# The last two expert tiles of an attention and mixture-of-experts kernel put behind a runtime condition

## The chip, the cores and the metric

The kernel runs on one core of one Trainium2 chip. The metric is the device time of one execution in microseconds (us). Three runs of the kernel before took 2227.67, 2231.09 and 2233.11 us; the median, 2231.09 us, is what the predicted time is set against.

## The reference

The input is 8 sequences of 1024 tokens with 256 features, all float32. First comes causal attention with 16 heads between two layer norms, with a residual. Then comes a mixture of experts:

```
logits = flat @ router_weight.T + router_bias
scores = softmax(logits);  topk_w, topk_idx = top_k(scores, 2)
gu   = flat @ gate_up_proj[e] + gate_up_bias[e]        # 8 experts, 256 -> 2 x 512
act  = (clip(up) + 1) * gate * sigmoid(1.702 * gate)   # gate cut at 7
down = act @ down_proj[e] + down_bias[e]               # 512 -> 256
out  = sum over the two chosen experts of down * topk_w
x    = x + layernorm(out)
```

The reference computes all experts for all tokens; what matters is each token's two chosen experts, so 8192 tokens make 16384 rows of expert work.

## The kernel before

**Sorting by expert.** While attention runs, `route` ranks the experts of every 512 tokens and scatters each token's normed row twice, into a DRAM buffer `xs_dram` that holds a region for each of the 8 experts. `counts` is how many rows each region has. From the counts, `table` (L279 and on) makes a list of 71 tiles on the chip: for tile i, `tables[..][0, 0, i]` is its expert and `tables[..][0, 1, i]` the row of `xs_dram` where its 256 rows (`TS`) begin. There are two such lists: one for the first 12 tiles (`EARLY`), made when 12 of the 16 groups of tokens are known and holding full tiles only, and one, `tables[NT]`, for the other tiles.

**Why 71.** `NTILES` (L100) is the most tiles that any routing can need: `(8192 * 2 - 8) // 256 + 8`. Each expert rounds its rows up to whole tiles, so the number of tiles with rows is between 64 and 71. A tile of the list that no expert takes gets expert 0 and the row `E * R` = 67584, a block behind all regions.

**One tile.** `load_tile` (L1257) has SyncE (SP) read the two numbers of the list into registers and start four loads: the rows `xs` (258 KB), the gate and up weights `wg` (1024 KB), the biases `bs` (132 KB), the down weights `wd` (512 KB). `turned` (L1284) transposes the rows on TensorE (PE), has ScalarE (ACT) copy them out of PSUM and has VectorE (DVE) work out to which rows of `yt_dram` the results go. `quarter` (L1303), four times, multiplies by a quarter of `wg` (line L1308) and makes a quarter of `act`: DVE takes gate and up out of PSUM (L1317, L1321), ACT does the sigmoid (L1319), GpSimd (POOL) multiplies (L1324), DVE finishes (L1329). `lower_half` (L1335) multiplies by `wd` (L1339), DVE adds the bias (`ys`, L1345), and POOL scatters the 2 x 128 result rows to `yt_dram` by two indirect DMAs (L1349).

**The order of the work.** It is written out by hand for PE, DVE and ACT. In the loop over tiles (L1453) the load of tile i + 2 is started at tile i (`AHEAD`), the transpose of tile i + 1 stands in quarter 2 of tile i, and `lower_half` of tile i - 1 is spread over the quarters of tile i (`behind`).

**The ends.** `both(t)` (L1359) closes group t of 512 tokens: it loads the attention result `x1` and the group's rows `yy` of `yt_dram`, sums the two experts' rows with their weights (ACT L1386, DVE L1391), takes mean and variance (L1395, L1396), the inverse root on POOL (L1403), `shift` on DVE (L1409), scales on ACT (L1416), adds on DVE (L1421), and writes 512 KB of output (L1425). It is a generator; `an_end` (L1449) runs one step of it inside a quarter. `tiles_for(r)` says from which tile on group r's rows are all done: 67 for group 14, 71 for group 15. Group 14's loads are put in the program when tile 67 ends, its steps begin at tile 69 (`i + 2`), and what is left of it runs after the loop. Group 15 (`final`) runs after the loop in any case; its four `yy` loads (L1372) wait for the last tile's scatters.

Of the kernel before, what the change touches and what calls it, by code (L numbers as in the profile page):

```python
# [11 lines left out]
F32 = mybir.dt.float32  # L12
# [5 lines left out]
P = 128  # L18
# [40 lines left out]
def attn_moe_kernel(  # L59
# [15 lines left out]
    nc = tc.nc  # L75
# [11 lines left out]
    E = router_w.shape[0]  # L87
    FF = down.shape[1]
    FT = FF // P
    TB = 512  # L90
    NT = B * S // TB
# [3 lines left out]
    TS = 256  # L95
    TN = TS // P
    R = B * S + TS
    ROWS = E * R + TS

    NTILES = (B * S * TOPK - E) // TS + E  # L100
# [84 lines left out]
    counts = const.tile([P, NT + 1, E], F32, name="counts")  # L185
# [66 lines left out]
    def fill_tails():  # L252
# [14 lines left out]
    tables = {  # L267
        n: const.tile([1, 2, NTILES], I32, name=f"table{n}") for n in (NT - LATE, NT)
    }
# [138 lines left out]
    with ExitStack() as attn:  # L408
# [653 lines left out]
        now = 0  # L1062
# [76 lines left out]
        with tc.manual_schedule(  # L1139
# [11 lines left out]
            for u in range(B * NG + 1):  # L1151
# [12 lines left out]
                for k in range(K):  # L1164
# [15 lines left out]
                    for pair in range(2):  # L1180
# [33 lines left out]
                        if len(late) > DELAY - 1 or (late and not second):  # L1214
                            f, kk = late[0]
# [22 lines left out]
            while late:  # L1238
                f, kk = late.popleft()
# [12 lines left out]
    m2 = pool("moe2", 2)  # L1252
# [4 lines left out]
    def load_tile(i):  # L1257
        tab = tables[NT - LATE if i < EARLY else NT]
        e = loaded(tab[:, 0, i : i + 1], E - 1)
        xs_sb = early.pop(i, None)  # L1260
        if xs_sb is None:
            at = loaded(tab[:, 1, i : i + 1], E * R)
            xs_sb = m4.tile([P, TN, XD], F32, tag="xs", name=f"xs_{i}")
            load = nc.sync.dma_start(out=xs_sb, in_=slot_rows(at))
            if i < EARLY:
                ahead_of(load, "xs")
        wg = m3.tile([P, KT, 2 * FF], F32, tag="wg", name=f"wg_{i}")
        nc.sync.dma_start(
            out=wg, in_=gate_up[ds(e, 1), :, :].rearrange("o (t p) f -> p (o t) f", p=P)
        )  # L1270
        bs = m4.tile([P, 2 * FT + D], F32, tag="bs", name=f"bs_{i}")
        nc.sync.dma_start(
            out=bs, in_=bias_dram[ds(e, 1), :, :].rearrange("o p c -> p (o c)")
        )
        wd = m4.tile([P, FT, D], F32, tag="wd", name=f"wd_{i}")
        nc.sync.dma_start(
            out=wd, in_=down[ds(e, 1), :, :].rearrange("o (t p) d -> p (o t) d", p=P)
        )
        return xs_sb, wg, bs, wd
# [4 lines left out]
    def turned(i, xs_sb):  # L1284
        ps = ps_x.tile([P, KT, TS], F32, tag="x", name=f"xtps_{i}")
        for kt in range(KT):
            for n in range(TN):
                nc.tensor.transpose(ps[:, kt, ts(n, P)], xs_sb[:, n, ts(kt, P)], ident)  # L1288
        xT = m2.tile([P, KT, TS], F32, tag="xsT", name=f"xsT_{i}")
        nc.scalar.copy(xT, ps)  # L1290

        far = m4.tile([P, TN], F32, tag="far", name=f"far_{i}")
        nc.vector.tensor_scalar(
            far, xs_sb[:, :, D], float(B * S * TOPK), float(i * (TS + 1)), ALU.is_ge, ALU.mult
        )
        nc.vector.scalar_tensor_tensor(
            far, xs_sb[:, :, D + 1], regions[NT - LATE if i < EARLY else NT][:, i : i + 1], far,
            ALU.not_equal, ALU.add,
        )
        nc.vector.tensor_tensor(places[:, i, :], far, xs_sb[:, :, D], ALU.add)  # L1300
        return xT

    def quarter(i, f, xT, wg, bs, act):  # L1303

        ps = ps_gu.tile([P, 2, TS], F32, tag="gu", name=f"gu_{i}_{f}")
        for half in range(2):
            for kt in range(KT):
                nc.tensor.matmul(  # L1308
                    ps[:, half, :],
                    lhsT=wg[:, kt, ds(half * FF + f * P, P)],  # L1310
                    rhs=xT[:, kt, :],
                    start=(kt == 0), stop=(kt == KT - 1),
                )
            if half == 0 and i + AHEAD < EARLY:
                pump(0.6, 0.35, 0.6, 0.35)
        gt = m3.tile([P, TS], F32, tag="gate", name=f"gate_{i}_{f}")
        nc.vector.tensor_scalar(gt, ps[:, 0, :], bs[:, f : f + 1], LIMIT, ALU.add, ALU.min)  # L1317
        sg = m3.tile([P, TS], F32, tag="sig", name=f"sig_{i}_{f}")
        nc.scalar.activation(sg, gt, AF.Sigmoid, scale=ALPHA)  # L1319
        up = m3.tile([P, TS], F32, tag="up", name=f"up_{i}_{f}")  # L1320
        nc.vector.tensor_scalar(  # L1321
            up, ps[:, 1, :], bs[:, FT + f : FT + f + 1], LIMIT + 1.0, ALU.add, ALU.min
        )
        in_order(nc.gpsimd.tensor_tensor(sg, sg, gt, ALU.mult))  # L1324
        if i + AHEAD < EARLY:
            pump(0.6, 0.35, 0.6, 0.35)

        def product():
            nc.vector.scalar_tensor_tensor(  # L1329
                act[:, f, :], up, 1.0 - LIMIT, sg, ALU.max, ALU.mult  # L1330
            )

        return product

    def lower_half(i, act, wd, bs):  # L1335
        ps = ps_b.tile([P, TN, D], F32, tag="b", name=f"dn_{i}")
        for n in range(TN):
            for f in range(FT):
                nc.tensor.matmul(  # L1339
                    ps[:, n, :], lhsT=act[:, f, ts(n, P)], rhs=wd[:, f, :],  # L1340
                    start=(f == 0), stop=(f == FT - 1),
                )
            yield
        y = m4.tile([P, TN, D], F32, tag="ys", name=f"ys_{i}")
        nc.vector.tensor_tensor(  # L1345
            y, ps, bs[:, 2 * FT :].unsqueeze(1).to_broadcast([P, TN, D]), ALU.add
        )
        for n in range(TN):
            put = nc.gpsimd.indirect_dma_start(  # L1349
                out=yt_dram[:, :],  # L1350
                out_offset=bass.IndirectOffsetOnAxis(ap=places[:, i, n : n + 1], axis=0),
                in_=y[:, n, :], in_offset=None,
            )
            in_order(put, scatter=True)
            apart(put, "yt")
        yield
# [70 lines left out]
    def tiles_for(r):  # L1427


        return max(((r + 1) * TB * TOPK - E) // TS + E, EARLY + E)  # L1430

    AHEAD = 2
    engines = mybir.EngineType
    with tc.manual_schedule(engines={engines.PE, engines.DVE, engines.Activation}):
        free[0] = False
        loads = {0: load_tile(0)}
        for i in range(IN_X, 2 * IN_X):
            at = loaded(tables[NT - LATE][:, 1, i : i + 1], E * R)
            early[i] = m4.tile([P, TN, XD], F32, tag="xs", name=f"xs_{i}")
            ahead_of(nc.sync.dma_start(out=early[i], in_=slot_rows(at)), "xs")  # L1440
        for i in range(1, AHEAD):
            loads[i] = load_tile(i)
        xTs = {0: turned(0, loads[0][0])}
        behind, left = None, None
        waiting = deque()
        ready = 0
        ends = deque()

        def an_end(i):  # L1449
            if ends and i >= ends[0][0] and next(ends[0][1], "end") == "end":  # L1450
                ends.popleft()

        for i in range(NTILES):  # L1453
            if i + AHEAD == EARLY:
                finish_all()
            if i + AHEAD < NTILES:
                loads[i + AHEAD] = load_tile(i + AHEAD)
            _, wg, bs, wd = loads.pop(i)
            xT = xTs.pop(i)
            act = m2.tile([P, FT, TS], F32, tag="act", name=f"act_{i}")  # L1460
            for f in range(FT):
                now_left = quarter(i, f, xT, wg, bs, act)
                if left:
                    left()
                left = now_left
                for _ in range(2 if f == FT - 1 and i % 2 else 1):
                    an_end(i)
                if f == 1 and behind:
                    next(behind)
                if f == 2:  # L1470
                    if i + 1 < NTILES:
                        xTs[i + 1] = turned(i + 1, loads[i + 1][0])
                    if behind:
                        next(behind)
                        next(behind)
                if i + AHEAD < EARLY:
                    pump(1.2, 0.7, 1.0, 0.7)
            while ready < NT and i >= tiles_for(ready):
                waiting.append(ready)
                ready += 1  # L1480
            if waiting and len(ends) < 2:
                work = both(routed[waiting.popleft()])
                next(work)
                ends.append((i + 2, work))
            behind = lower_half(i, act, wd, bs)
        left()
        for _ in behind:
            pass
        for r in [*waiting, *range(ready, NT)]:
            ends.append((0, both(routed[r], r == NT - 1)))  # L1490
        while ends:
            an_end(NTILES)
        free[0] = True
# [36 lines left out]
```

## Time and profile before

| what | value |
|---|---|
| median of three runs | 2231.09 us (2227.67 to 2233.11) |
| time of the profiled execution | 2227.21 us |
| its span, first to last instruction | 2225.5 us |
| PE busy | 2161.5 us, 97% of the span |
| DVE, ACT, POOL busy | 1647.3, 1090.8, 1067.0 us |
| mean granted PE clock | 0.994 of full speed |
| gate and up matmuls, L1308 | 2272 in 71 tiles, 516.2 us busy |
| down matmuls, L1339 | 1136 in 71 tiles, 273.5 us busy |

The page gives times in us from the start of the span. A busy share is an average over the whole span; a stage is read by cutting the span into windows. The chain of waits follows the execution back from its last instruction, each time to what released it.

The two stages show in the page's forty slices of 55.6 us: in the first 25, attention, the loads move 12 to 59 GB/s after the first slice; in the next 14, the expert tiles, 178 to 273 GB/s; the last holds the end of the tiles and the last group.

### The profile page before, as it was taken

Reading aid. Unit: us, or ns where it says so; the run is one execution under the profiler, and the core shown is the slowest. Engines: PE = TensorE matmul, PEld = TensorE weight load, DVE = VectorE, ACT = ScalarE, POOL = GpSimd, SP = SyncE. Lnnn points to the kernel's source line nnn. Section 1 sums busy time; section 2 is a strip of 40 time slices with the busy share of each in tenths; the row PEclk is TensorE's granted clock in tenths of the full one; section 3 lists DMA queues with packets and bytes.
Section 4 is the critical chain, followed back from the end, with each engine's and each line's share of the span. In section 5 each row is a group of like instructions: output and inputs, shape, how many; then the busy total and the mean of one; then the engine's idle time right before and its main releaser. Section 6 shows DMA issues by size and latency. Waiting matters only on the chain.

```text
span 2225.5 us, 45180 instructions
## 1 busy us (share of the span) xinstructions
PE 2161.5 (97%) x16801; PEld 1347.5 (61%) x16801; DVE 1647.3 (74%) x3770; ACT 1090.8 (49%) x2179; POOL 1067.0 (48%) x1229
## 2 busy tenths in 40 slices
PE   7999999999999999999999999999999999999995
PEld 3444544544544445445445444778888888888885
DVE  4776777867867777877776787676668888887775
ACT  3666665665666666666666666431122322322222
POOL 3421652662573573473472463464444444444543
PEclk9999999999999999999999999999999999999998
DMA  4001102102102111111111111657667778777773
GB/s 106 17 12 35 26 16 55 40 21 59 40 21 55 36 30 38 52 30 31 49 40 23 45 52 40 219 178 253 214 227 269 259 262 273 266 243 273 241 245 124
DMA packets 141363, 251.17 MB, mean 113 GB/s; under 512 B 17664, under 2 KB 103576, under 8 KB 139224
## 3 DMA queue, kind: packets, MB, share of 16 engines
q1 hardware_dynamic: 126968, 212.17, 30.5%
q0 software_dynamic: 12960, 35.54, 4.2%
q8 instruction: 133, 2.18, 0.4%
q14 instruction: 86, 0.70, 0.1%
q10 hardware_dynamic: 1216, 0.58, 0.1%
HBM read 175.74 MB, written 55.76 MB: 104 GB/s over the span
## 4 chain that ended last, share of the span: by engine, by line
PE 81%; DVE 10%; POOL 4%; issue 3%; ACT 1%; DMA 1%; SPq 0%; ACTq 0%; DVEq 0%; POOLq 0%
PE sa L693 20%; PE gu L1308 17%; PE av L825 12%; PE dn L1339 9%; PE sb L788 7%; PE yps L886 3%; PE pjq L600 3%; PE pjk L600 3%; PE vps L586 2%; PE avt L856 1%; DVE acc L1391 1%; PE xtps L1288 1%; DVE gate L1317 1%; DVE act L1329 1%; DVE up L1321 1%
## 5 line engine op out<-in xcount | busy, mean ns | idle before, releaser
L796 ACT ACTIVATE pT<-sb 128x512 f32<-128x512 f32 x1152 | 625.2, 595 | 404.5 <-PE sb L788 375.7
L788 PE MATMUL sb<-qP,kP 32*128 32x512 f32 (+3 forms) x3072 | 710.7, 523 | 2.1 <-DMA qP<-nmT 1.0
L693 PE MATMUL sa<-kP,qP 32*128 32x512 f32 (+3 forms) x3072 | 653.8, 524 | 3.4 <-DVE mx L703 1.4
L1308 PE MATMUL gu<-xsT,wg 128*128 128x256 f32 x2272 | 516.2, 379 | 0.8 <-ACT xsT L1290 0.7
L1308 PEld LDWEIGHTS gu<-xsT,wg 128*128 128x128 f32 x2272 | 430.6, 190 | 59.9 <-ACT xsT L1290 1.4
L805 POOL TENSOR_SCALAR_AFFINE_SELECT pT<-pT 128x512 f32<-128x512 f32 x256 | 160.0, 641 | 592.3 <-ACT pT L796 586.9
L709 DVE TENSOR_REDUCE mx<-sa 128x2 f32<-128x1024 f32 x256 | 311.5, 1219 | 112.2 <-PE sb L788 108.6
L1319 ACT ACTIVATE sig<-gate 128x256 f32<-128x256 f32 x284 | 118.3, 417 | 562.7 <-DVE gate L1317 560.7
L825 PE MATMUL av<-pT,vpad 128*32 128x256 f32 (+1 forms) x5120 | 345.0, 366 | 1.1 <-DVE avs L836 0.9
L1324 POOL TENSOR_TENSOR sig<-sig,gate 128x256 f32<-128x256 f32 x284 | 210.6, 743 | 274.9 <-ACT sig L1319 273.0
L693 PEld LDWEIGHTS sa<-kP,qP 32*128 32x128 f32 x3072 | 227.8, 184 | 188.4 <-issue 97.3
L788 PEld LDWEIGHTS sb<-qP,kP 32*128 32x128 f32 x3072 | 297.6, 184 | 40.9 <-ACT pT L796 7.2
L825 PEld LDWEIGHTS av<-pT,vpad 128*32 128x32 f32 x5120 | 116.4, 108 | 287.2 <-issue 208.0
L1339 PE MATMUL dn<-wd,act 128*128 128x256 f32 x1136 | 273.5, 381 | 8.0 <-DVE act L1329 7.5
L1317 DVE TENSOR_SCALAR gate<-gu,bs 128x256 f32<-128x256 f32 x284 | 135.7, 478 | 154.2 <-PE gu L1308 138.1
L1339 PEld LDWEIGHTS dn<-wd,act 128*128 128x128 f32 x1136 | 208.6, 190 | 40.7 <-DVE act L1329 16.0
L703 DVE CUSTOM_DVE_ANT_0 sa<-sa,cmask 128x512 f32<-128x512 f32 x256 | 178.1, 697 | 51.2 <-PE sb L788 27.0
L1349 POOL DMA_INDIRECT ytd<-ys,places x142 | 142.9, 1006 | 136.5 <-DVE ys L1345 112.3
L1046 POOL DMA_INDIRECT xsd<-xn,slots x128 | 126.9, 992 | 47.0 <-issue 29.4
L718 DVE TENSOR_REDUCE mx<-sa 128x2 f32<-128x512 f32 x128 | 88.1, 689 | 75.5 <-PE sb L788 49.7
L1329 DVE SCALAR_TENSOR_TENSOR act<-up,sig 128x256 f32<-128x256 f32 x284 | 131.7, 464 | 14.5 <-POOL sig L1324 14.5
L1321 DVE TENSOR_SCALAR up<-gu,bs 128x256 f32<-128x256 f32 x284 | 134.5, 474 | 0.0
(204 smaller groups left out, 2399.9 us busy)
## 6 DMA issues: line engine op xcount, KB each, us to landing
wg<-_L_ffn_gate_up_proj_dram SPq DMA_DIRECT2D x71, 1024.0 KB
wd<-in_L_ffn_down_proj_dram SPq DMA_DIRECT2D x71, 512.0 KB
xs<-xsd SPq DMA_DIRECT2D x67, 258.0 KB
yy<-ytd SPq DMA_DIRECT2D x15, 1024.0 KB
bs<-biasd SPq DMA_DIRECT2D x71, 132.0 KB
x<-in_L_attn_x_dram SPq DMA_DIRECT2D x16, 512.0 KB
x1d<-y SPq DMA_DIRECT2D x16, 512.0 KB
x<-x1d SPq DMA_DIRECT2D x16, 512.0 KB
```

Of the source, the lines that this page charges most:

```text
L693: nc.tensor.matmul(ps[:, hh, ds(at, w)], lhsT=qP[r, ts(i, P)], rhs=kP[r, ds(c * QC, w)], start=True, stop=True,)
L703: nc.vector.tensor_tensor_reduce(out=ps[:, hh, :], in0=ps[:, hh, :], in1=cmask, scale=1.0, scalar=NEG, op0=ALU.add, op1=ALU.max, accum_out ...
L709: nc.vector.tensor_reduce(mx[:, heads, i, 2:3], ps, AX.X, ALU.max)
L788: nc.tensor.matmul(banks[hh][:, ds(at, QC - off)], lhsT=kP[r, ts(j, P)], rhs=qP[r, ds(c * QC + off, QC - off)], start=True, stop=True,)
L796: nc.scalar.activation(pT[:, 2 * pair + hh, :], banks[hh], AF.Exp)
L805: in_order(nc.gpsimd.affine_select(out=d, in_=d, compare_op=ALU.is_ge, fill=0.0, base=0, pattern=[[0, HG], [1, P]], channel_multiplier=-1,))
L825: nc.tensor.matmul(av[ds(hh * HS, HS), ds(off + a - at, z - a)], lhsT=vp[:, j, ds((g * HG + hh) * VS, HS)], rhs=pT[:, hh, a:z],  start=c n ...
L1308: nc.tensor.matmul(ps[:, half, :], lhsT=wg[:, kt, ds(half * FF + f * P, P)], rhs=xT[:, kt, :], start=(kt == 0), stop=(kt == KT - 1),)
L1317: nc.vector.tensor_scalar(gt, ps[:, 0, :], bs[:, f : f + 1], LIMIT, ALU.add, ALU.min)
L1321: nc.vector.tensor_scalar(up, ps[:, 1, :], bs[:, FT + f : FT + f + 1], LIMIT + 1.0, ALU.add, ALU.min)
L1324: in_order(nc.gpsimd.tensor_tensor(sg, sg, gt, ALU.mult))
L1339: nc.tensor.matmul(ps[:, n, :], lhsT=act[:, f, ts(n, P)], rhs=wd[:, f, :], start=(f == 0), stop=(f == FT - 1),)
```

## The change

The loop over tiles ends two tiles earlier, at `SURE` = 69, and nothing is loaded or transposed ahead for tiles 69 and 70 in it. Behind the loop, `values_load` has every engine read one number into a register, the row where tile 69 begins by `tables[NT]`. If it is less than `E * R`, tiles 69 and 70 run one after the other by a new function `tile_alone`, without loads ahead and without steps of other work between. Otherwise they are jumped over. What is left of the ends then runs as before.

```diff
+    SPARE = 2
+    SURE = NTILES - SPARE
+
+    def tile_alone(i):
+        xs_sb, wg, bs, wd = load_tile(i)
+        xT = turned(i, xs_sb)
+        act = m2.tile([P, FT, TS], F32, tag="act", name=f"act_{i}")
+        last = None
+        for f in range(FT):
+            now = quarter(i, f, xT, wg, bs, act)
+            if last:
+                last()
+            last = now
+        last()
+        for _ in lower_half(i, act, wd, bs):
+            pass
...
-        for i in range(NTILES):
+        for i in range(SURE):
...
-            if i + AHEAD < NTILES:
+            if i + AHEAD < SURE:
...
-                    if i + 1 < NTILES:
+                    if i + 1 < SURE:
...
         left()
         for _ in behind:
             pass
+        spare = nc.values_load(
+            tables[NT][:, 1, SURE : SURE + 1], min_val=0, max_val=E * R,
+            skip_runtime_bounds_check_because="tables made on the chip from counts of tokens",
+        )
+        with tc.If(spare < E * R):
+            for i in range(SURE, NTILES):
+                tile_alone(i)
         for r in [*waiting, *range(ready, NT)]:
             ends.append((0, both(routed[r], r == NT - 1)))
```

In the built program, each engine's list now has a register load and a compare-and-branch behind tile 68, then the block of the two tiles (51 instructions on DVE, 21 on ACT, 15 on POOL, 23 on SP), then a second block that runs in its place: it raises the semaphores by what the two tiles would have raised them (two instructions on PE, DVE and ACT each, five on POOL, ten on SP), after waits for what came before, and ends with a branch to the rest. On SP those waits are for all its earlier DMAs, on POOL for earlier scatters. The arithmetic steps of group 14, of which tiles 69 and 70 held nearly all, now stand in the rest, behind the branch; its loads stay where they were, in tile 68's time.

## The prediction

> **What bounds the kernel now.** First the page: who is busy, and whose time the chain of waits is made of.
>
> ```profile
> PE 2161.5 (97%) x16801; PEld 1347.5 (61%) x16801; DVE 1647.3 (74%) x3770; ACT 1090.8 (49%) x2179; POOL 1067.0 (48%) x1229
> PE 81%; DVE 10%; POOL 4%; issue 3%; ACT 1%; DMA 1%; SPq 0%; ACTq 0%; DVEq 0%; POOLq 0%
> ```
>
> PE bounds nearly all of it. But the change lies at the end, so I cut the end into stages: tile 68, 69 and 70 (from the end of one tile's third quarter of L1308 to the next's), what is left of tile 70, the trip of its rows to DRAM and back, and the last group.
>
> ```profile
> 2166.80:2177.60 10.80, 10.80 (x54) 9.51 (x53) 7.34 (x17) 2.14 (x5) 5.28 (x7) 1.00 0.72 239
> 2177.60:2188.40 10.80, 10.80 (x54) 9.51 (x53) 8.66 (x22) 3.34 (x8) 4.46 (x6) 1.00 0.47 163
> 2188.40:2199.11 10.71, 10.62 (x50) 9.03 (x48) 8.94 (x22) 2.07 (x5) 6.66 (x8) 1.00 0.07 24
> 2199.11:2205.31 6.20, 4.15 (x17) 2.68 (x15) 2.31 (x6) 2.38 (x5) 2.21 (x3) 1.00 0.12 42
> 2205.31:2213.64 8.33, 0.00 (x0) 0.00 (x0) 1.41 (x5) 0.00 (x0) 1.97 (x2) 0.77 0.48 157
> 2213.64:2225.50 11.86, 0.00 (x0) 0.00 (x0) 6.26 (x20) 4.21 (x8) 1.59 (x2) 0.50 0.25 89
> ```
>
> Columns: length, then busy us of PE, weight loads, DVE, ACT, POOL, then clock, DMA share, GB/s. A tile costs 10.8 us, all of it PE. Then PE is done, and in the fifth stage nearly everything waits for the round trip of the last rows. The timeline shows its ends:
>
> ```profile
> 2204.62 0.69 DVE L1345 TENSOR_TENSOR ys<-dn,bs 128x512 f32<-128x512 f32 x1 [2.52 <-PE dn L1339]
> 2205.59 1.01 POOL L1349 DMA_INDIRECT ytd<-ys,places  x1 [3.95 <-DVE ys L1345]
> 2206.91 0.96 POOL L1349 DMA_INDIRECT ytd<-ys,places  x1 [0.30 <-issue]
> 2210.29 1.74 SPq L1372 DMA_DIRECT2D yy<-ytd  x4
> 2213.64 0.51 ACT L1386 ACTIVATE acc<-yy,chosen_w 128x256 f32<-128x256 f32 x1 [11.30 <-DMA yy<-ytd]
> ```
>
> Call the end of the last tile's `ys` T0. Scatter, landing, load and landing take 2213.64 - 2205.31 = 8.33 us, whatever tile is the last.
>
> **Is the condition false?** No row of the profile tells it: an empty tile loads and computes as a full one does. I worked the routing out from the reference and its inputs. The experts get 1887, 2102, 2059, 1860, 1869, 2468, 1692 and 2447 rows, so 8+9+9+8+8+10+7+10 = 69 tiles of 256. The early list takes only full tiles, so it adds none. Tiles 69 and 70 are empty, and 92 rows would have to change expert before any of these counts passed its next multiple of 256.
>
> **What goes.** Tiles 69 and 70: 10.80 + 10.71 = **21.51 us**, the second and third rows above. The same 8.33 us behind the last tile stays, with tile 68 in tile 70's place. The loads of the two tiles (about 1.9 MB each) go too, but loads were not late there: PE was busy 10.80 of 10.80 us.
>
> **What is added: the branch.** Each engine reads a register from the list, compares, branches, raises semaphores and branches again. The register read has rows on SP:
>
> ```profile
> L244 SPq TENSOR_LOAD <-table x142: 262/275/990, 1319.9 to 2159.0; - x142
> ```
>
> 0.28 us in the median. Raising a semaphore is the 0.02 to 0.05 us of the trace's EVENT_SEMAPHORE records. A taken branch has no row. From below it is about such a record, 0.02 us. From above it is a stop until code has come by DMA, and code does come so:
>
> ```profile
> q8 instruction: 133, 2.18, 0.4%
> q14 instruction: 86, 0.70, 0.1%
> ```
>
> 133 packets carry 2.18 MB, 16 KB each; 86 carry 0.70 MB, 8 KB each. The trace has 34176 records on PE (16801 matmuls, 17375 of weight loads and waits), 257 for each packet of the one kind, and 11004 on the other engines, 128 for each of the other. So code comes in blocks of 256 and 128 instructions. An 8 KB packet takes 0.31 to 0.89 us; with its request I set it at the 2.5 us that a scatter of this stage takes from issue to landing, 2.9 us together, an estimate. Which end? The jump skips 51 instructions on DVE, 21 on ACT, 15 on POOL and 23 on SP, less than half a block, so its target lies in the block that runs or in the next, which straight code needs early as well. I take the lower end, 0.05 us a branch: 0.28 + 2 x 0.05 + 0.05 = 0.43 us an engine, and keep 2 x 2.9 + 0.28 + 0.05 = 6.1 us for the range.
>
> [...]
>
> **What hides it.** On PE nothing follows. SP waits in its second block for all its earlier DMAs; the last of these, `yy` and `x1` of group 14, are issued at 2174.12 and 2175.64, in tile 68. ACT used that `yy` at 2180.48 without a wait, and now 0.6 MB of loads that shared the queue with it are gone. SP's next task is the `yy` load of group 15 at T0 + 4.98, that is 2188.8 in old time: over 8 us of cover. POOL ends its second scatter at T0 + 2.56 and must raise its semaphores before that same load: 2.42 us of cover for 0.5 us (a semaphore raise by the software queue took 0.03 us at the kernel's start). Only DVE and ACT can show it.
>
> **What is moved: group 14.** Its sums lay in tiles 69 and 70, beside PE. Now they come behind the branch, beside the 8.33 us trip. ACT's four `acc` need only `yy` and end before T0: 2180.48 + 4 x 0.52 = 2182.6, against T0 = 2205.31 - 21.51 = 2183.80. From T0 on, with durations of the last group's rows:
>
> - DVE's branch: 0.43
> - four rounds of L1391, L1395, L1396 (2214.19 to 2218.79): 4.60
> - `ve`, then POOL: 0.26 to its start, and 1.04 for `rstd` of four columns (the row at 2194.03): 1.30
> - `shift` and its two hand-overs: 0.30
> - four `o` on ACT (the row at 2200.28, x4): 2.06
>
> Sum 8.69 us; ACT then begins group 15's `acc` at T0 + 8.69 in place of T0 + 8.33, 0.36 late. DVE's fourth addition of group 14 and the stretch of an `acc` beside a scatter (0.76 for 0.48 at 2190.79) add some tenths in one place; I take **0.5 us late** in all. The 512 KB output of group 14 is written under group 15's 11.86 us.
>
> **Sum.** -21.51 + 0.5 = -21.0 us. The profiled execution took 2227.21 us, 1.7 above its span; with the change 2206.2. It was 3.9 us below the median of the runs shown, under their lowest. Set against the median: 2231.09 - 21.0 = **2210.1 us**.
>
> **The rivals.**
>
> *Code stalls at the branches.* One block late on DVE or ACT gives 8.69 + 2.9 - 8.33 + 0.1 = 3.4 us late, 2213.0 us; both late, 6.3 us, 2215.9 us. The same holds if POOL's semaphores come after its 2.42 us of cover. [...] Against: the short jump.
>
> *The tiles run after all* (slower; the change then does not skip what it says). One mechanism: an expert's count passes a multiple of 256, the list has 70 tiles with rows, and both tiles run alone. Loads begin only behind the branch: 1.9 MB at the 268 GB/s of the tile stage, 7.2 us. Each tile is then a chain with nothing beside it: transposes and copy 1.2, four quarters of 1.73, and the 6.20 us of the fourth row above, 14.3 us. Both: 7.2 + 28.6 = 35.8 in place of 21.51, 14.3 us more: about 2245.9 us. It decides from the 70th tile; I count 69.
>
> *The exposed group costs more than a tail.* If DVE ran its rounds at the 0.95 us that L1391 takes in the median beside POOL, four times 0.47 more: 2.4 us late, 2212.0 us. Against: POOL has only two scatters there.
>
> **How the numbers follow.** Forecast 0.78; code stalls 0.13; dearer group 14 0.05; the tiles run 0.03; something else 0.01. Bounds: nothing late gives 2209.6; both blocks late 2215.9. The runs before lie 3.4 below and 2.0 above their median, which I add in part: 2206 to 2217.5. Measurement can tell about 0.3%, 6.7 us, from no change. All cases but the third and last are at least 15 us faster: faster 0.95, same 0.01, slower 0.04.
>
> **What would show it.** 138 instead of 142 scatters of L1349 and 69 loads of `wg`; T0 near 2183.8; on DVE a gap under 0.5 us between `ys` and group 14's first L1391; the `yy` load of L1372 still 4.98 us after T0; group 15's first `acc` at T0 + 8.6 to 8.9. Wrong would be a gap of 2 us or more on DVE, ACT or POOL at the branch, or L1372 late behind POOL.

## The result and the profile after

The changed kernel took 2206.68 us in the median (four runs, 2204.11 to 2212.08); the kernel before, in the same comparison, 2229.38 us (2226.53 to 2233.11). The ratio is 0.9899, 95% interval 0.9884 to 0.9914: 22.5 us less, 19.2 to 25.9. The forecast was 2210.1 us, 21.0 less.

The page of the changed kernel, busy times and then the chain by engine:

```profile
PE 2143.1 (97%) x16697; PEld 1330.8 (60%) x16697; DVE 1633.1 (74%) x3738; ACT 1086.1 (49%) x2169; POOL 1055.7 (48%) x1217
DVE 0%; ACT 0%; issue 0%; POOL 0%; ACTq 0%; DVEq 0%
```

PE lost 18.4 us of busy time. The chain is of no use here: followed back from the end it comes to DVE's branch, finds no releaser, and stops, so it holds only the last stretch. The windows of the end, cut as before: the last tile (now 68) from its first matmul of L1308 on, what is left of it behind its last one, the trip of its rows, the last group.

```profile
2170.37:2180.73 10.36, 10.36 (x50) 9.12 (x48) 6.40 (x14) 1.67 (x4) 5.39 (x7) 1.00 0.62 221
2180.73:2186.87 6.14, 4.15 (x17) 2.68 (x15) 2.32 (x5) 2.12 (x5) 2.14 (x3) 1.00 0.16 58
2186.87:2195.08 8.21, 0.00 (x0) 0.00 (x0) 5.58 (x18) 1.98 (x4) 3.18 (x3) 0.64 0.39 129
2195.08:2206.90 11.82, 0.00 (x0) 0.00 (x0) 6.71 (x22) 4.20 (x9) 1.57 (x2) 0.50 0.32 111
```

The last three stood at 6.20, 8.33 and 11.86 us: each is about as long as before, and ahead of them are two stages fewer. The last tile itself took 10.71 us before (tile 70) and takes 10.36 now. What changed is the filling: DVE now works 5.58 us of the trip's window (1.41 before), on group 14. The timeline, the same five steps as before:

```profile
2186.18 0.69 DVE L1345 TENSOR_TENSOR ys<-dn,bs 128x512 f32<-128x512 f32 x1 [2.52 <-PE dn L1339]
2187.15 1.01 POOL L1349 DMA_INDIRECT ytd<-ys,places  x1 [3.95 <-DVEq L1512]
2188.46 1.14 POOL L1349 DMA_INDIRECT ytd<-ys,places  x1 [0.30 <-issue]
2191.14 1.75 SPq L1372 DMA_DIRECT2D yy<-ytd  x4
2195.08 2.40 ACT L1386 ACTIVATE acc<-yy,chosen_w 128x256 f32<-128x256 f32 x4
```

T0, the end of the last `ys`, is 2186.87. The load starts at T0 + 4.27 (4.98 before), group 15's first `acc` at T0 + 8.21 (8.33).

The two profiled spans differ by 18.6 us only, 2225.5 to 2206.9. The end accounts for more: the three tile stages before took 10.80 + 10.80 + 10.71 = 32.31 us, the one that is left 10.36, and 21.95 + 0.06 + 0.12 + 0.04 = 22.2 us. The missing 3.6 arose ahead of the tiles, in code that the change leaves alone: ACT's first `xsT` came at 1404.7 before and 1408.4 after, and the granted clock of the whole run was 0.994 and 0.992. Two spans from one execution each are a poor measure of 20 us; the stages at the end are a good one.

### The profile page after: what moved, and what is told of

Same layout as the page of the kernel before. It is cut to its first block, busy times and chain, and to the rows that moved or that the text cites. A ratio compares the mean times of both kernels' runs of the same rounds, so it can differ in the third digit from the quotient of the medians.

```text
span 2206.9 us, 44890 instructions
## 1 busy us (share of the span) xinstructions
PE 2143.1 (97%) x16697; PEld 1330.8 (60%) x16697; DVE 1633.1 (74%) x3738; ACT 1086.1 (49%) x2169; POOL 1055.7 (48%) x1217
## 5 line engine op out<-in xcount | busy, mean ns | idle before, releaser
L1308 PE MATMUL gu<-xsT,wg 128*128 128x256 f32 x2208 | 501.7, 379 | 0.8 <-ACT xsT L1290 0.7
L1308 PEld LDWEIGHTS gu<-xsT,wg 128*128 128x128 f32 x2208 | 418.4, 190 | 58.2 <-ACT xsT L1290 1.4
L1324 POOL TENSOR_TENSOR sig<-sig,gate 128x256 f32<-128x256 f32 x276 | 204.2, 742 | 268.8 <-ACT sig L1319 266.9
L1339 PE MATMUL dn<-wd,act 128*128 128x256 f32 x1104 | 265.6, 381 | 7.8 <-DVE act L1329 7.4
L1339 PEld LDWEIGHTS dn<-wd,act 128*128 128x128 f32 x1104 | 202.8, 190 | 39.4 <-DVE act L1329 15.4
L1329 DVE SCALAR_TENSOR_TENSOR act<-up,sig 128x256 f32<-128x256 f32 x276 | 128.3, 465 | 14.3 <-POOL sig L1324 14.3
```

Source lines behind the costliest of these rows:

```text
L1308: nc.tensor.matmul(ps[:, half, :], lhsT=wg[:, kt, ds(half * FF + f * P, P)], rhs=xT[:, kt, :], start=(kt == 0), stop=(kt == KT - 1),)
L1339: nc.tensor.matmul(ps[:, n, :], lhsT=act[:, f, ts(n, P)], rhs=wd[:, f, :], start=(f == 0), stop=(f == FT - 1),)
```

## Experiments

**The changed kernel again (no edit).**

> The changed kernel unaltered, to narrow its ratio to the kernel before. If the gain is the PE time of two tiles (21.5 us) and nothing else, the ratio is 0.990 to 0.991 (2229.4 - 21.5 = 2207.9 us). If fewer loads or a higher granted clock add to it, it is below 0.989. From the end of the last ys (T0) the group 15 load L1372 should start at T0 + 4.3 and its first acc at T0 + 8.2, as in the first profile of it.

Ratio 0.9891 (0.9873 to 0.9909), on a chip where the kernel before took 2267.72 us: 24.7 us less, 20.6 to 28.8. T0 + 4.27 and T0 + 8.21 came back to the hundredth. The 22.2 us of the end lie in both intervals; whether up to 2.5 us more is won is not settled by these.

**No branch.**

```diff
-        spare = nc.values_load(
-            tables[NT][:, 1, SURE : SURE + 1], min_val=0, max_val=E * R, ...
-        )
-        with tc.If(spare < E * R):
-            for i in range(SURE, NTILES):
-                tile_alone(i)
```

> The changed kernel without register load and condition: tiles 69 and 70 are left out whatever the list says. Theory (branch hidden): DVE's 0.36 us between ys and group 14's first acc goes, at most that much is won, under 0.02%; time within 1 us of the changed kernel's. Rival (the branch stalls some engine): 2 us or more faster than the changed kernel, and L1372 clearly earlier than T0 + 4.3.

Ratio 0.9891 (0.9872 to 0.9910), the same as with the branch. The trace resolves what the time cannot, against the kernel run again on this chip: the load at T0 + 4.06 in place of 4.27, the first `acc` at T0 + 7.76 in place of 8.21, the end of the span at T0 + 19.59 in place of 20.08. **The branch costs 0.45 to 0.5 us here**: 0.44 on DVE (its first L1391 at T0 + 0.36 in place of T0 - 0.08), and 0.2 on POOL's second scatter, 1.14 us in place of 0.96. The rival of 2 us or more falls.

**Only the tail: 71 tiles, no branch, group 14's steps behind the loop.**

```diff
-                ends.append((i + 2, work))
+                ends.append((i + 2 if i < 67 else NTILES, work))
```

> The kernel before with all 71 tiles and no branch, but with group 14's arithmetic steps moved behind the loop, as the change does. By the prediction's step: group 15's first acc is about 0.3 us late, total +0.3 to +0.5 us. By the changed kernel's trace: the output write of group 14 no longer lies beside the last scatters' landing, so L1372 starts at T0 + 4.3 in place of T0 + 4.98, and the total moves by -0.3 to +0.2 us. If the earlier L1372 came from the missing loads of tiles 69 and 70 instead, it stays at T0 + 4.98 here.

Ratio 0.9996 (0.9977 to 1.0014). From T0 (2248.06): the load at 4.04, the first `acc` at 7.76, the end at 19.57, all earlier than in the kernel before (4.98, 8.33, 20.18), though all 71 tiles are there. So the earlier load does not come from the missing loads of two tiles. The last tile is shorter too, 10.36 us as in the changed kernel, with nothing jumped; in the kernel before, a weight load for `dn` waits there 0.49 us for DVE, which is working on group 14. So that gain comes from the moved steps. The last tile's window with the moved steps, then the timeline of that run's end, then the wait in the kernel before:

```profile
2231.55:2241.91 10.36, 10.36 (x49) 9.13 (x48) 5.53 (x13) 1.67 (x4) 5.01 (x7) 1.00 0.07 25
```

```profile
2247.37 0.69 DVE L1345 TENSOR_TENSOR ys<-dn,bs 128x512 f32<-128x512 f32 x1 [2.52 <-PE dn L1339]
2252.09 1.76 SPq L1372 DMA_DIRECT2D yy<-ytd  x4
```

```profile
2193.39 0.30 PEld L1339 LDWEIGHTS dn<-wd,act 128*128 128x128 f32 x2 [0.49 <-DVE act L1329]
```

**Is it group 14's output write?** Two cuts of the kernel before's DMA view, 2207.0 to 2209.2 (q1 and q0) and 2209.2 to 2210.3 (q0), show the order of packets: the 512 KB write (q1) and the first scatter (q0), and only then the second scatter, although POOL had issued it by 2207.9.

```profile
q1 hardware_dynamic: 489, 0.50, 67.8%
q0 software_dynamic: 48, 0.13, 19.7%
...
```

```profile
q0 software_dynamic: 48, 0.13, 33.5%
```

The first attempt to move the write:

```diff
+            while held:
+                held.pop()()          # behind group 15's yy loads
...
-            nc.sync.dma_start(out=out_t[t][:, g], in_=o[:, g])
+            if t == routed[NT - 2]:
+                held.append(lambda: nc.sync.dma_start(out=out_t[t], in_=o))
+            else:
+                nc.sync.dma_start(out=out_t[t][:, g], in_=o[:, g])
```

> The kernel before, all 71 tiles, no branch, all arithmetic where it was; only the issue of group 14's output write is moved from ahead of group 15's yy loads to behind them. If that write is what delayed the landing of the last scatters, L1372 starts at T0 + 4.0 to 4.3 in place of T0 + 4.98 and the first acc 0.7 to 0.9 us earlier; the whole is within 0.1% of the kernel before. If something else moved with group 14 did it, L1372 stays at T0 + 4.98.

The write did not move. SP's order is not written by hand, and in the built program the write still stood ahead of the loads, so this run says nothing on the cause (ratio 0.9995, 0.9986 to 1.0004):

```profile
2205.55 0.69 DVE L1345 TENSOR_TENSOR ys<-dn,bs 128x512 f32<-128x512 f32 x1 [2.52 <-PE dn L1339]
2207.68 0.40 SPq L1428 DMA_DIRECT2D out_dram<-o  x1
2211.22 1.74 SPq L1372 DMA_DIRECT2D yy<-ytd  x4
```

The second attempt ties the write to the last load:

```diff
+                tc.add_manual_dep(put.ins, last_load.ins.name, ...)
```

> As the kernel with the later write was meant: the kernel before with 71 tiles, no branch and its arithmetic in place, but SP now does issue group 14's 512 KB output write behind group 15's four yy loads (in the run before this one the write still stood ahead of them). If the write's packets, which in the trace of before lie between those of the last two scatters, are what delayed the second scatter, that scatter's packets end near T0 + 3.5 in place of 4.5, L1372 starts near T0 + 4.05 in place of 4.98, and group 15's first acc at about T0 + 7.7 in place of 8.33. If not, L1372 stays at T0 + 4.98.

```profile
2244.89 0.69 DVE L1345 TENSOR_TENSOR ys<-dn,bs 128x512 f32<-128x512 f32 x1 [2.52 <-PE dn L1339]
2249.63 1.76 SPq L1372 DMA_DIRECT2D yy<-ytd  x4
2251.49 0.39 SPq L1435 DMA_DIRECT2D out_dram<-o  x1
```

T0 is 2245.58: the load starts at T0 + 4.05, 0.93 us earlier, the first `acc` at T0 + 7.18 (7.7 was expected), the end at T0 + 19.44 in place of 20.18. Between 2247.5 and 2249.7 now both scatters lie, 88 of their 96 packets and none of q1:

```profile
q0 software_dynamic: 88, 0.23, 29.5%
```

So it was the write. (One execution; its 2266.73 us against 2260.8 of one of the kernel before says nothing about 0.7 us.)

**The two tiles run after all.** First with a condition that is always true:

```diff
-        with tc.If(spare < E * R):
+        with tc.If(spare < E * R + 1):
```

> The condition made true always, so the two tiles run alone behind the branch. By the prediction's rival: loads start behind the branch, 7.2 + 2 x 14.3 = 35.8 us over the changed kernel, about 2243 us. By what the trace of the changed kernel shows, SP reaches its branch 10 us before DVE does, so the loads are hidden and only the two chains count: 2 x 13.6 = 27 us over the changed kernel, about 2234 us, 5 to 6 us slower than the kernel before.

The built program has neither register read nor branch left, since no value can fail the condition, so this is the price of the two lone tiles by themselves. `ys` of tile 68 ends at 2226.03, of tile 70 at 2252.40: 26.37 us, where leaving them out moved T0 by 21.95 + 0.06 = 22.0. SP issued their loads from 2215.99 on, 10 us ahead. Ratio 0.9998 (0.9977 to 1.0019), too wide to tell 4 us. Then with a real branch, by the row of a tile that has rows:

```diff
-            tables[NT][:, 1, SURE : SURE + 1], ...
+            tables[NT][:, 1, SURE - 1 : SURE], ...
```

> The condition now reads the row of tile 68, which has rows, so it is true when the kernel runs, and the two tiles run alone behind a real branch. Theory from the traces so far: SP reaches its branch some 9 us before DVE, its loads are hidden, and the chains of the two tiles take 2 x 13.2 us (26.4 in the run without a branch) in place of 21.5, less what the tail wins; with some 0.4 us for the branch, 4 to 5.5 us slower than the kernel before, ratio 1.002. By the prediction's rival (loads begin behind the branch): 14.3 us slower, ratio 1.0064.

Ratio 1.0016 (1.0007 to 1.0025): 3.6 us slower than before, 1.6 to 5.6. The timeline, SP's first load and the starts of the two lone tiles on PE, with `ys` of the tile before each:

```profile
2173.80 0.39 SPq L1264 DMA_DIRECT2D xs<-xsd  x1
...
2182.34 0.60 PE L1288 MATMUL xtps<-ident,xs 128*128 128x128 f32 x4
2182.54 0.69 DVE L1345 TENSOR_TENSOR ys<-dn,bs 128x512 f32<-128x512 f32 x1 [2.52 <-PE dn L1339]
...
2195.53 0.60 PE L1288 MATMUL xtps<-ident,xs 128*128 128x128 f32 x4
2195.73 0.69 DVE L1345 TENSOR_TENSOR ys<-dn,bs 128x512 f32<-128x512 f32 x1 [2.52 <-PE dn L1339]
...
2208.91 0.69 DVE L1345 TENSOR_TENSOR ys<-dn,bs 128x512 f32<-128x512 f32 x1 [2.52 <-PE dn L1339]
```

Each lone tile takes 13.19 us. From tile 68's first matmul of L1308 (2166.73, and 2166.80 in the kernel before) it is 62.5 us to the end of the span, before 58.7: 3.8 more, close to the measured 3.6.

**How long may the jump be?** The jumped block written two, four and six times; none of it runs. (Twice and four times are one execution each: 2208.03 and 2208.08 us.)

```diff
-            for i in range(SURE, NTILES):
+            for i in [*range(SURE, NTILES)] * 6:     # 2, 4
```

> The jumped block made six times as long (the two tiles written six times; the condition is false, nothing of it runs): 306 instructions on DVE, 126 on ACT, 90 on POOL, 138 on SP. Theory (code comes in blocks of 128 on these engines, the running one and the next are at hand): DVE's target is now outside, so DVE stops for a fetch, 1 to 3 us between its compare and group 14's first acc in place of 0.36 us, and the whole is up to 3 us slower than the changed kernel; POOL, with 90, stays quick. Rival (a branch costs the same at any length): gap and time as in the changed kernel.

> The jumped block written twice: 102 instructions on DVE, 42 on ACT, 30 on POOL, 46 on SP, none of which run. Theory (code in blocks of 128 on these engines, the running block and the next at hand): the target still lies in the next block, the gap on DVE from compare to the next instruction stays near 0.16 us. Rival (any longer jump costs more): it grows.

> The jumped block written four times: 204 instructions on DVE, 84 on ACT, 60 on POOL, 92 on SP. By the theory the target on DVE is in the next block or the one behind it, by where the branch stands in its own block; a stop of about 3.1 us, as with 306, or none (0.16 us). On ACT and POOL, under 128, no stop. Rival (cost grows with length): about two thirds of 3.1 us.

Group 14's first L1391 on DVE, with what held it, in the changed kernel and with the block twice, four and six times as long:

```profile
2187.23 0.48 DVE L1391 SCALAR_TENSOR_TENSOR acc<-yy,chosen_w,acc 128x256 f32<-128x256 f32 x1 [0.36 <-DVEq L1512]
```

```profile
2185.17 0.49 DVE L1391 SCALAR_TENSOR_TENSOR acc<-yy,chosen_w,acc 128x256 f32<-128x256 f32 x1 [0.71 <-DVEq L1512]
```

```profile
2186.20 0.48 DVE L1391 SCALAR_TENSOR_TENSOR acc<-yy,chosen_w,acc 128x256 f32<-128x256 f32 x1 [3.00 <-DVEq L1512]
```

```profile
2226.08 0.48 DVE L1391 SCALAR_TENSOR_TENSOR acc<-yy,chosen_w,acc 128x256 f32<-128x256 f32 x1 [3.30 <-DVEq L1512]
```

From the trace's records, the us from the end of an engine's compare to its next instruction, by instructions jumped:

| | x1 | x2 | x4 | x6 |
|---|---|---|---|---|
| DVE (51, 102, 204, 306) | 0.16 | 0.51 | 2.80 | 3.10 |
| ACT (21, 42, 84, 126) | 0.13 | 0.13 | 0.42 | 0.42 |
| POOL (15, 30, 60, 90) | 0.14 | 0.14 | 0.14 | 0.45 |
| SP (23, 46, 92, 138) | 0.46 | 0.46 | 0.46 | 5.22 |

It is a step, not a slope: at most 0.51 us up to 126 instructions jumped, 2.8 us and more at 138 (SP), 204 and 306 (DVE). A cost in proportion to length falls: 204 cost nearly what 306 do. The 0.16 us expected of twice the length was missed, by 0.35. On PE the compare itself took 0.375 us, and 3.36 to 3.80 with the longer blocks. The two tiles hold 104 matmuls and as many weight loads, so PE did not stop for some 208 instructions and did for twice as many.

Code comes during the stop. The DMA view of the 2.8 us between DVE's compare and its next instruction, with the block four times as long, has an 8 KB packet of code; that of the 2.8 us after T0 in the changed kernel has the scatter's packets and nothing else:

```profile
q14 instruction: 1, 0.01, 0.7%
```

```profile
q0 software_dynamic: 48, 0.13, 13.1%
```

By the trace's records such a packet starts 0.97 us after DVE's compare ended, with four and with six times the length, and DVE goes on 1.5 and 1.6 us after it has come.

Length alone does not decide. With 92 instructions jumped, SP went on after 0.46 us but stopped 4.4 us between its fifth semaphore instruction and its sixth, which the changed kernel passes in 0.08; no run shows why. Both stops of SP end at T0 - 4.9, when group 14's loads are done in the other runs, so how much of its 5.22 us is the jump's own is open.

With the block two, four and six times as long the span ends at T0 + 21.77, 23.08 and 23.02, in the changed kernel at T0 + 20.07; the ratio of the longest, on another chip, is 0.9928 (0.9905 to 0.9950). Of the 1.7 us that the double jump costs, DVE's longer gap explains 0.35: its load L1372 starts at T0 + 6.48, for a reason of its own that the last section gives.

**Branches where PE is the bound: 71 tiles, eight false conditions in the tile loop.**

```diff
+            if i in (20, 26, 32, 38, 44, 50, 56, 62):
+                row = nc.values_load(tables[NT][:, 1, NTILES - 1 : NTILES], ...)
+                with tc.If(row < E * R):
+                    nc.vector.memset(dummy, 0.0)
```

> The kernel before with all 71 tiles, and eight false conditions in the middle of the tile loop, one behind each of tiles 20, 26, ... 62, each jumping over one small fill on DVE. Here PE is the bound and nothing drains. If a branch costs PE its register load and compare (0.49 + 0.38 us in the changed kernel's trace), it is 8 x 0.9 = 7 us, 0.3% slower than before. If PE's sequencer runs ahead of its array and hides it: under 1 us. If a branch empties the pipeline of the engines: 8 x 3 = 24 us or more, 1% slower.

Ratio 1.0003 (0.9985 to 1.0021): 0.7 us for eight, between 3.4 less and 4.8 more. 7 us are out, and 24 with them. The view of the condition's line shows PE's compare; a window around the second one (1746 to 1750) shows that PE did not pause there:

```profile
L1493 PEldq COMPARE_BRANCH  x8: 202/202/228, 1681.9 to 2141.1; - x8
```

```profile
1746.00:1750.00 4.00, 4.00 (x23) 3.52 (x22) 3.85 (x10) 1.30 (x3) 2.48 (x3) 1.00 0.94 296
```

PE's sequencer read the register (0.30 us in the median of the eight) and compared (0.20 us) while matmuls kept PE busy for 4.00 of the window's 4.00 us.

## Why the prediction was right, and where its sizes were off

**What goes** was right in kind, two stages of PE-bound tiles, and 0.44 us short: 21.95 in place of 21.51. The sum let tiles 69 and 70 go and kept tile 68 at 10.80 us, but the tile that is last now takes 10.36, without the wait that group 14 had put into tile 70 (PE busy 10.62 of its 10.71 us). The windows were also cut otherwise than said, from the first matmul of L1308 of one tile to the next one's; the lengths stand. The scatters went from 142 to 138.

**The condition** was false, as the count of 69 tiles said: nothing of the block ran.

**The branch** was mis-sized in its parts, not in its sum. On DVE the gap is 0.36 us and the cost, by the run without a branch, 0.44, against 0.43. The register read took longer than SP's 0.28, but lay beside `ys`; the view of its line, and two lines of the condition's:

```profile
L1508 DVEq TENSOR_LOAD <-table x1: 544/544/544, 2186.2 to 2186.2; - x1
```

```profile
L1512 DVEq COMPARE_BRANCH  x1: 72/72/72, 2186.8 to 2186.8; - x1
...
L1512 POOLq INC_SWDGE_SEM  x1: 1277/1277/1277, 2187.9 to 2187.9; - x1
```

For POOL, "a semaphore raise by the software queue took 0.03 us at the kernel's start" was a poor row: here it took 1.28. POOL's cover of 2.42 us from its second scatter's end held because its sequencer reached the branch during the scatters: it was through at 2189.21, T0 + 2.34. SP was through at 2182.01, 9 us before its load, as said.

**Code stalls**, the rival at 0.13, did not occur, and the runs show why: the stop is real, at 2.8 to 3.1 us a jump on DVE (set at 2.9), but 51 instructions do not reach it. Blocks of 128, the estimate from the packets, fit where DVE stops: with 204 and 306 instructions jumped (2.80 and 3.10 us), not with 51 and 102 (0.16 and 0.51). That the block behind the running one is always at hand was an assumption, and no run shows it. Without a stop the compare-and-branch took 45 to 72 ns, and 202 to 375 on PE.

**Group 14** is the term that was wrong in sign. "I take 0.5 us late in all"; group 15's `acc` came 0.12 early. Two parts: the sum to T0 + 8.69 came out at 8.21, since its four rounds took 4.34 and not 4.60 (the row they were taken from held an extra `ve` and waits for loads), the branch's gap 0.07 less and the rest 0.15 less; and the bound that they were held against moved. I took the 8.33 us trip as fixed, "whatever tile is the last", but 0.9 us of it was group 14's own write lying ahead of the last scatter, and the change moves that write out of the way. I counted the write at its new place and not what it had cost at its old one. With the step moved alone the last tile is 0.35 us shorter and the tail 0.6; the branch takes 0.5 of that back. Both size errors point the same way, and together they are the 1.2 us between the 21.0 of the forecast and the 22.2 of the stages; the rest of the measured 22.5 is within the noise.

**The two tiles run** was priced 14.3 us slower; it is 3.6 (1.6 to 5.6). The step that failed: "Loads begin only behind the branch", 7.2 us. True, but SP's branch is its own, and SP came to it 9 to 10 us before DVE's T0. And each tile takes 13.2 and not 14.3 us, mostly since PE begins the second's transposes 0.9 us before the first's `ys` ends. (14.3 us more than the median of 2231.09 are 2245.4, not 2245.9; and the chances call this rival the third case, where it is the fourth of their list.)

**Left open:** the measured 22.5 and 24.7 us lie 0.3 to 2.5 above the 22.2 of the stages; the intervals hold 22.2. From the first `xsT` to the end of the span it is 820.8 us in the kernel before, 798.6 in the changed one and 798.7 when it ran again, so these traces show nothing further won among the tiles, such as from the 3.9 MB of loads that are gone. They are single executions, and others were some 3 us longer there: 781.6 to T0 without the branch, 778.5 with it.

## What to carry to other kernels

Work for a worst case that the data do not need can be jumped at run time, here for about half a microsecond, if the jump is short on the engines that others wait for (51 instructions cost DVE 0.44 us, 204 stopped it for 2.80). Each engine branches by itself, and one with slack need not show: SP was through at 2182.01, 9 us before its next load. Check the price of the other way too: here it is 3.6 us when the tiles are needed, against 22 won when they are not; how often they are needed was worked out for one input only. When a step moves, count what its transfers stood in front of at the old place, here 0.93 us; a bound taken from the old trace may hold them.

## What the runs showed of the hardware that was not expected

- A 512 KB write that SP issued at 2206.75 in the kernel before, while POOL had the last indirect scatter (2206.91 to 2207.87) still to make, delayed the load behind that scatter by 0.93 us (T0 + 4.98 with the write ahead, 4.05 with it behind).
- Raising the semaphores of the software DMA queue took POOL 1.27 to 1.28 us in each run that jumped over the tiles, and 0.03 at the program's start.
- With the block written twice, its eight scatters in the built program cover all eight of that queue's semaphores, the two still pending included. POOL's second block then waits for the last scatters to land and raises the semaphores afterwards; the load L1372, which waits for that, comes at T0 + 6.48 in place of 4.27, by 4.05 us of waiting. With four and six times the length the wait is 3.16 and 2.75 us and the load comes at T0 + 5.59 and 5.48, there hidden behind DVE's stop:

```profile
L1512 POOLq EVENT_SEMAPHORE  x5: 17/43/4052, 2185.3 to 2185.6; - x5
```

- The register read took 0.49 to 0.54 us on PE, DVE, ACT and POOL where each did its first one, and 0.28 to 0.31 us in the median of eight.
